# Letting convolution taps in by a backlog meter, and resting buffer rings behind their stores, in a four-layer image kernel

## The chip, the cores and the metric

The kernel runs on one core of one Trainium2 chip. The metric is the device time of one execution in microseconds (us), as the median of several runs. A core has five engines that work from queues of their own, each in order: PE (matrix products and transposes), DVE (vector operations), ACT (activations, copies), POOL (elementwise work) and SP. Nearly all DMAs of this kernel, loads and stores alike, are issued from SP's queue. Data lie in SBUF, sums of products in PSUM, and intermediate images in DRAM.

## The reference

The input is four images of 384 channels and 48 x 48 pixels (2304 tokens), all float32. Four residual layers follow each other, each on the group-normalised image:

```python
x = x + _L0_conv_ref(_gn(x), ...)   # Mamba block: in-projection, causal conv of 4 taps, SiLU,
                                    # scan h = dA*h + dBx over 2304 tokens for 768 channels x 16 states,
                                    # y = sum_s h*C + xin*D, gate by SiLU(z), out-projection, layer norm
x = x + _L1_conv_ref(_gn(x), ...)   # 1x1 conv, filter in the DFT of 8x8 patches,
                                    # depthwise 3x3 conv (9 taps), gelu(x1)*x2, 1x1 conv
x = x + _L2_conv_ref(_gn(x), ...)   # depthwise 11x11 conv, kernels made of 4 points
x = x + _L3_conv_ref(_gn(x), ...)   # 4 experts (two 1x1 convs each), top-2 gate per pixel
```

Where every expert is picked first and second somewhere in the batch, the weights of the top 2 become 1, so that the usual case of layer 3 is the plain sum of the four experts; a branch at the end (`weighted`) does the general case and is not taken with these inputs.

## The kernel before, in words

The scan of layer 0 sets the clock of the program. Each image is cut into 5 chunks of tokens (`CHUNKS`, 460 or 464), each chunk into 6 blocks of 128 channels times 16 states: 96 scans of 128 x 460 per chunk, 1920 in all. The loop `for u in range(N + 6)` in `scans` emits one scan per **slot** `u` under `tc.manual_schedule()`, so each engine's instructions stand in the order in which the loop writes them. In each slot stand: ACT's `decay` two or three slots ahead (da = exp(dt*A), in PSUM), POOL's `drive` three slots ahead (bu = u*B), DVE's `scan`, and the product with C. The product is on DVE in a "fast" slot (`product_now`) and on POOL in a "slow" one (`product`); after the first image's chunks, slots with `u % 4 < 2` are slow. PE then adds the 16 states up by transposing (`turned`). B and C of two slots are broadcast from DRAM to all partitions by one DMA each (`spread`, SP; 3 buffers for B, 4 for C).

All other work is written as generators (`Task`) that yield what they will do next: `("pe", weight, (ring, 1))`, `("act",)`, `("dve",)`, `("late",)`, `("pool",)`. A `Lane` steps its tasks three times per slot: phase 0 (act), 1 (pe, dve, pool), 2 (late). A `Meter` holds PE's work: its value falls by 2.3 us per slot, and a step of a nonzero weight is let in only up to 3.7. A `Ring` stands for a set of buffers; its oldest buffer counts as free as soon as `done` was called, which is when the last instruction that uses it has been emitted.

The lanes are `aux` (layer 0's own projections and layer norms, planned by slot), `start` (z of images 2 and 3, early), `one` (layers 1 and 2 and the scores of layer 3, `later`) and `two` (`experts` of layer 3). Layers 1 to 3 of image b run beside the scans of image b+1, from slot 480(b+1)+42 on. So the first 480 slots carry layer 0 alone, the last image's layers 1 to 3 come after the scans, and what is left of image 2's experts is done there too. That last part is called the **tail** here; in it the slot loop is no longer tied to scans.

Parts that the change touches:

- `taps` in `finish_strip` (layer 1, L1400 to L1420): nine taps per 128 channels of a strip of 8 image rows (24 strips in all images), 27 taps a strip, each one DVE instruction of 128 x 384. It lets 2 taps into a slot, 3 if the slot is slow.
- `block` (layer 3): one expert on 144 tokens, two products of 9 matmul calls. Image strips come as `xe` from `x3d`, the running sum as `ye` from `y3d`. For the first expert the sum is written over `xe`; later ones write over `ye`. Both rings have 2 buffers during the scans. The store (L1791) is emitted in the slot after its DVE add.
- `windows` and `load_band` (layer 2): bands of `xb` from `x2d` (L1513), stored to `x3d` (L1582), 2 buffers.
- `residual` (L1095) stores layer 0's result out of `xch`, and `load` (L731) refills the other tile of that name for the next chunk. `early_z` (L661) stores z from 3 buffers.
- `begin1` loads layer 1's output weights for each image in two parts.

Of the kernel before, what the change touches and what calls it, by code (L numbers as in the profile page):

```python
# [9 lines left out]
F32 = mybir.dt.float32  # L10
# [32 lines left out]

class Ring:


    def __init__(self, make, n):
        self.make, self.n, self.read = make, n, []

    def free(self, k=1):  # L50
        return all(self.read[: max(0, len(self.read) + k - self.n)])
# [6 lines left out]
    def done(self, k):  # L58
        self.read[k] = True


class Meter:


    def __init__(self, each, limit):
        self.each, self.limit, self.value = each, limit, 0.0

    def slot(self, given):
        self.value = max(0.0, self.value - self.each) + given
# [25 lines left out]
class Lane:  # L95
# [7 lines left out]
    def step(self, phase, slot, at=0):  # L103
        for task in self.active:
            if task.ended:
                continue
            kind, weight, ring, when = task.next
            if PHASE.get(kind, 1) != phase or task.after > slot:
                continue
            if weight and self.bound and self.meter.value + weight > self.meter.limit:  # L110
                continue
            if (ring and not ring[0].free(ring[1])) or (when and not when()):
                continue
            self.meter.value += weight
            task.move(slot)
        self.active = [t for t in self.active if not t.ended]
        while (
            self.queue and len(self.active) < self.width and self.queue[0].at <= max(at, slot)
            and all(t.ended for t in self.queue[0].needs)
        ):  # L120
            task = self.queue.pop(0)
            task.move()
            if not task.ended:
                self.active.append(task)

    def drain(self, slot, others=()):
        n = 0
        while self.queue or self.active:
            self.meter.value = 0.0
            for phase in range(3):  # L130
                for lane in (self, *others):
                    lane.step(phase, slot + n, 1 << 30)
            n += 1
            assert n < 20000, "stuck"
# [8 lines left out]
def tile_layers(ctx: ExitStack, tc: tile.TileContext, a: dict, out: bass.AP):  # L143
# [22 lines left out]
    gexp = const("gexp", [GROUPS, C], a["c_gexp"])  # L166
# [8 lines left out]
    def group_norm(st, bank, mean, rstd, name):  # L175

        mv = small.tile([P, CT, 2], F32, name=f"mv{name}", tag="mv")
        for ct in range(CT):
            nc.vector.bn_aggr(mv[:, ct, :], st[:, ct].rearrange("p k s -> p (k s)"))

        def to_groups(src, n, what):
            ps = bank(f"g{what}{name}")
            for ct in range(CT):
                nc.tensor.matmul(
                    ps[:GROUPS, :n], lhsT=gsel[:, ct, :], rhs=src(ct),
                    start=ct == 0, stop=ct == CT - 1,
                )
            return ps[:GROUPS, :n]

        def to_channels(src, n, what):  # L190
            ps = bank(f"c{what}{name}")
            for ct in range(CT):
                nc.tensor.matmul(
                    ps[:, n * ct : n * ct + n], lhsT=gexp[:, bass.ts(ct, P)], rhs=src,
                    start=True, stop=True,
                )
            return ps[:, : n * CT]

        grp = small.tile([GROUPS, 2], F32, name=f"grp{name}", tag="grp")
        nc.vector.tensor_copy(grp, to_groups(lambda ct: mv[:, ct, :], 2, "m"))  # L200
        nc.vector.tensor_copy(mean, to_channels(grp[:, 0:1], 1, "m"))
        dev = small.tile([P, CT], F32, name=f"dev{name}", tag="dev")
        nc.vector.tensor_sub(dev, mv[:, :, 0], mean)
        nc.vector.tensor_mul(dev, dev, dev)
        var = small.tile([GROUPS, 1], F32, name=f"var{name}", tag="var")
        nc.vector.scalar_tensor_tensor(
            var, to_groups(lambda ct: dev[:, ct : ct + 1], 1, "v"), GN_EPS, grp[:, 1:2],
            ALU.add, ALU.add,
        )
        nc.gpsimd.tensor_tensor(var, var, neghalf[:GROUPS, 0:1], ALU.pow)  # L210
        nc.vector.tensor_copy(rstd, to_channels(var, 1, "v"))

    def group_norm_steps(st, ring, mean, rstd, name):
# [15 lines left out]
        def to_channels(src, n, what):  # L229
            ps, k = ring.take(f"c{what}{name}")  # L230
            for ct in range(CT):
                nc.tensor.matmul(
                    ps[:, n * ct : n * ct + n], lhsT=gexp[:, bass.ts(ct, P)], rhs=src,
                    start=True, stop=True,
                )
            return ps[:, : n * CT], k
# [179 lines left out]
    with ExitStack() as first:  # L416
# [55 lines left out]
        stats0 = wp.tile([P, 2, CT, 2, 3, 6], F32, name="stats0")  # L472
# [86 lines left out]
        def scans(wk, mm, ring, meter, place, lanes, begin):  # L559
# [9 lines left out]
            def image_stats(b, ct, h):  # L569
# [4 lines left out]
                for k in range(3):  # L574
                    yield ("dve",)
                    nc.vector.bn_stats(stats0[:, b % 2, ct, h, k, :], t[:, bass.ts(k, LB)])

            def image_norm(b):
                yield from group_norm_steps(
                    stats0[:, b % 2].rearrange("p c h k s -> p c (h k) s"), ring,  # L580
# [4 lines left out]
            def early_stats(b, ct, h):  # L585
# [6 lines left out]
                for k3 in range(3):  # L592
                    yield ("dve",)
# [9 lines left out]
            def early_fold(b):  # L603
# [21 lines left out]
                yield ("dve",)  # L625
# [11 lines left out]
            def early_z(b, t, j):  # L637
# [22 lines left out]
                yield ("pool",)  # L660
# [28 lines left out]
            def fold(b, which):  # L689
# [22 lines left out]
                yield ("dve",)  # L712
# [12 lines left out]
            def load(i):  # L725
                (b, t), c = G[i], st[i]
# [8 lines left out]
                return  # L735
                yield

            def project(i, j):
# [27 lines left out]
                yield ("dve",)  # L766
# [74 lines left out]
            def steps(i, p):  # L841
# [22 lines left out]
                yield ("dve",)  # L864
# [146 lines left out]
            def gate(i, m):  # L1011
# [9 lines left out]
                yield ("late",)  # L1021
# [4 lines left out]
            def out_proj(i, k):  # L1026
# [20 lines left out]
                yield ("dve",)  # L1047
# [4 lines left out]
            def layer_norm(i):  # L1052
# [8 lines left out]
                yield ("dve",)  # L1061
# [12 lines left out]
            def residual(i, ct):  # L1074
# [14 lines left out]
                yield ("dve",)  # L1089
# [4 lines left out]
                yield ("pool",)  # L1094
# [81 lines left out]
            for tag, shape, n in (  # L1176
# [7 lines left out]
                    n,  # L1184
# [14 lines left out]
            with tc.manual_schedule():  # L1199
# [10 lines left out]
                for u in range(N + 6):  # L1210
# [17 lines left out]
                    meter.slot(0.44)  # L1228
                    soon = u % PAIR >= 8
# [25 lines left out]
                while aux.queue or aux.active:  # L1255
                    at += 1
                    meter.slot(0.0)
                    for phase in range(3):
# [5 lines left out]

        def slow_slot():
            return place[0] % 4 < 2

        def later(b, ring, accr):
# [11 lines left out]
            def slots(tag, shape, n):  # L1280

                return Ring(
                    lambda name: d["wk"].tile(shape, F32, name=name, tag=tag, bufs=n), n
# [11 lines left out]
            def begin1():  # L1295
# [3 lines left out]
                w = d["w_out"] = wk.tile([P, 2, C], F32, name=f"w_out1_{b}", tag="w_out", bufs=1)  # L1299
                nc.sync.dma_start(w[:, 0, :], a["L1_w_outT"][:P, :])  # L1300
                nc.sync.dma_start(w[64:P, 1, :], a["L1_w_outT"][P:, :])
# [38 lines left out]
            def patches(hb, wb):  # L1340
# [24 lines left out]
                yield ("late",)  # L1365
# [27 lines left out]
            def finish_strip(hb):  # L1393
# [7 lines left out]
                def taps(ct):  # L1401
# [3 lines left out]
                    room = 3 if slow_slot() else 2  # L1405
                    for k in range(9):
                        if not room:
                            yield ("dve",)
                            room = 3 if slow_slot() else 2
                        room -= 1  # L1410
# [18 lines left out]
                yield ("dve",)  # L1429
# [6 lines left out]
                yield ("dve",)  # L1436
# [3 lines left out]
                for ct in range(CT):  # L1440
# [3 lines left out]
                        ps[:, :LB], lhsT=w[:, 0, bass.ts(ct, P)], rhs=act[:, 0, :],  # L1444
# [3 lines left out]
                        ps[:, :LB], lhsT=w[64:P, 1, bass.ts(ct, P)], rhs=act[64:P, 1, :],  # L1448
                        start=False, stop=True,
                    )  # L1450
                    yield ("late",)
# [26 lines left out]
            xbs = slots("xb", [P, max(BANDS) * W], 2)  # L1478
# [68 lines left out]
            def windows(ct, k, r, first, last, final):  # L1547
# [26 lines left out]
                if last:  # L1574
                    yield ("late",)
# [5 lines left out]
                    yield ("pool",)  # L1581
# [40 lines left out]
            xg = slots("xg", [P, CT, LB], 2)  # L1622

            def begin3():
# [16 lines left out]
                yield ("dve",)  # L1641
# [4 lines left out]
            def scores_of(hb):  # L1646
# [23 lines left out]
                yield ("dve",)  # L1670
# [17 lines left out]
        def experts(b, ring, rings):  # L1688
# [15 lines left out]
            def begin(e):  # L1704
# [21 lines left out]
                yield ("late",)  # L1726
# [4 lines left out]
            def load3(s, e):  # L1731
                yield (
                    "pool", 0, None,
                    lambda: rings["xe"].free() and (not e or rings["ye"].free()),
                )
                x = take(("x", s, e), "xe", f"xe{b}_{s}_{e}")
                nc.sync.dma_start(x, strip(x3d[b], bass.ts(s, EB)))
                if e:
                    y = take(("y", s, e), "ye", f"ye{b}_{s}_{e}")
                    nc.sync.dma_start(y, strip(y3d, bass.ts(s, EB)))  # L1740
                yield from wait(3)

            def block(s, e):
# [33 lines left out]
                yield ("late",)  # L1777
                key = ("y" if e else "x", s, e)
                x = d[key][0]
                if e:  # L1780
                    y = x.rearrange("p c t -> p (c t)")
                    nc.vector.tensor_add(y, ps[:, : CT * EB], y)  # L1782
                else:
                    for m in range(CT):
                        nc.vector.scalar_tensor_tensor(
                            x[:, m, :], ps[:, bass.ts(m, EB)], b2_sum[:, m : m + 1],
                            x[:, m, :], ALU.add, ALU.add,
                        )
                ring.done(r)
                yield ("pool",)  # L1790
                nc.sync.dma_start(strip(out[b] if e == NE - 1 else y3d, bass.ts(s, EB)), x)  # L1791
                done(key)
# [106 lines left out]
        def of_experts(pool, sizes):  # L1899
            for tag, n in sizes.items():  # L1900
# [5 lines left out]
                    n,  # L1906
# [11 lines left out]
        meter = Meter(2.3, 3.7)  # L1918
        one, two = Lane(8, meter), Lane(4, meter)

        def begin(b):
# [10 lines left out]
            {"we": 1, "xe": 2, "ye": 2, "hr": 1},  # L1932
        )
        with (
# [7 lines left out]
            while not all(ring.read):  # L1942
# [6 lines left out]
        with (  # L1949
# [4 lines left out]
            of_experts(wk, {"we": 2, "xe": 3, "ye": 3, "hr": 3})  # L1954

            one.queue += later(NB - 1, ring, accr)
            while one.queue or one.active or two.queue or two.active:
                at += 1
                meter.slot(0.0)
                if not (one.queue or one.active):  # L1960
# [124 lines left out]
```

## Time and profile before

| | us |
|---|---|
| median of 3 runs | 5413.93 (5412.89 to 5417.67) |
| profiled execution, whole | 5405.14 |
| its span, first to last instruction | 5403.1 |
| first and last scan start | 86.5 and 4515.3 |

| engine | busy us | share of the span |
|---|---|---|
| PE, matmuls | 4646.1 | 86% |
| PE, weight loads | 3666.7 | 68% |
| DVE | 4067.1 | 75% |
| POOL | 3363.1 | 62% |
| ACT | 2989.0 | 55% |

A share of the whole span mixes stages of different limits, so the profile is read by stage here: a stretch with layer 1's taps, one with layer 2, one with experts, and the tail. The trace's record of the 1920 scans on DVE also gives each slot its place in time: slot u begins where the u-th scan starts. From slot 384 to 480, with layer 0 alone, a slot took 1.95 us; over the 96 slots from 1056 on it took 2.85 us.

### The profile page before, as it was taken

How to read it: one execution, taken by the hardware profiler on the slowest of the kernel's cores; microseconds unless marked ns; L12 is line 12 of the kernel's file. 1: busy time of each engine (PE TensorE's matmuls, PEld its weight loads, DVE VectorE, ACT ScalarE, POOL GpSimd, SP SyncE). 2: the span in 40 equal slices, each digit the busy share in tenths (PEclk: the TensorE clock that was granted, in tenths of full speed). 3: DMA queues.
4: the chain of work that ended last, by engine and by line, in shares of the span. 5: the costliest groups of instructions: out<-in, count | busy, mean ns of one | idle time of the engine just before them, and what ended most of it. 6: DMA issues, size and time to landing. Idle time of an engine off the chain costs nothing. (4 is left out here: it accounts for less than half of the span.)

```text
span 5403.1 us, 82006 instructions
## 1 busy us (share of the span) xinstructions
PE 4646.1 (86%) x27796; PEld 3666.7 (68%) x27796; DVE 4067.1 (75%) x5581; ACT 2989.0 (55%) x6632; POOL 3363.1 (62%) x3020
## 2 busy tenths in 40 slices
PE   5898877787768988888889988888799988999899
PEld 3555545454446766765668867665678877889799
DVE  5998899889997888889887778798987875452200
ACT  3566655565547765565567745565477653335321
POOL 3788778886677788876678678775677783000000
PEclk8898987788879999998899999998899999999899
DMA  4565545443344555655566565655566573543210
GB/s 152 172 187 175 178 128 150 129 143 120 111 127 131 148 165 157 191 161 147 149 172 178 161 200 155 173 146 149 154 182 174 158 213 115 175 138 105 64 27 23
DMA packets 648873, 794.36 MB, mean 147 GB/s; under 512 B 60149, under 2 KB 642661, under 8 KB 648062
## 3 DMA queue, kind: packets, MB, share of 16 engines
q1 hardware_dynamic: 638148, 787.38, 49.9%
q8 instruction: 221, 3.62, 0.3%
q10 hardware_dynamic: 10298, 1.67, 0.2%
q14 instruction: 206, 1.69, 0.1%
HBM read 685.04 MB, written 103.81 MB: 146 GB/s over the span
## 5 line engine op out<-in xcount | busy, mean ns | idle before, releaser
L953 POOL TENSOR_TENSOR bu<-u,B 128x460 f32<-128x460 f32 (+1 forms) x1920 | 2227.0, 1170 | 795.5 <-DVE g L966 349.8
L942 ACT ACTIVATE da<-dt,a_neg 128x460 f32<-128x460 f32 (+1 forms) x1920 | 1242.4, 648 | 310.6 <-DVE g L986 185.6
L886 PE MATMUL y<-ident,g 128*115 128x128 f32 (+1 forms) x7680 | 1111.3, 292 | 192.5 <-DVE g L986 114.8
L886 PEld LDWEIGHTS y<-ident,g 128*115 128x115 f32 (+1 forms) x7680 | 991.2, 183 | 400.4 <-DVE g L986 140.5
L995 POOL TENSOR_TENSOR g<-g,C 128x460 f32<-128x460 f32 (+1 forms) x885 | 1030.0, 1164 | 246.8 <-ACT carry L980 244.3
L966 DVE TENSOR_TENSOR_SCAN da<-da,carry,bu 128x460 f32<-128x460 f32 (+1 forms) x828 | 971.7, 1174 | 122.2 <-ACT da L942 76.7
L966 DVE TENSOR_TENSOR_SCAN g<-da,carry,bu 128x460 f32<-128x460 f32 (+1 forms) x708 | 819.8, 1167 | 57.7 <-issue 18.8
L986 DVE TENSOR_TENSOR g<-da,C 128x460 f32<-128x460 f32 (+1 forms) x1035 | 656.4, 634 | 175.7 <-DMA C<-bcd 62.0
L980 ACT COPY carry<-da 128x1 f32<-128x1 f32 x828 | 130.3, 157 | 760.5 <-DVE g L986 758.0
L1750 PE MATMUL pout<-hr,we 128*128 128x144 f32 x3456 | 485.0, 297 | 51.5 <-ACT hr L1766 37.8
L1750 PE MATMUL ph<-xe,we 128*128 128x144 f32 x3456 | 484.7, 298 | 33.6 <-DMA xe<-x3d 18.9
L1750 PEld LDWEIGHTS pout<-hr,we 128*128 128x128 f32 x3456 | 456.3, 197 | 75.3 <-ACT hr L1766 47.9
L1750 PEld LDWEIGHTS ph<-xe,we 128*128 128x128 f32 x3456 | 459.4, 199 | 51.5 <-DMA xe<-x3d 13.7
L1557 PE MATMUL pc<-band,row 128*128 128x162 f32 (+14 forms) x3456 | 451.3, 284 | 11.2 <-ACT row L1544 10.9
L1557 PEld LDWEIGHTS pc<-band,row 128*128 128x128 f32 x3456 | 440.0, 194 | 16.6 <-ACT row L1544 11.9
L749 PE MATMUL pin<-xch,w_inx 128*128 128x463 f32 (+2 forms) x720 | 344.8, 621 | 55.1 <-DMA xch<-in_x 32.3
L1415 DVE SCALAR_TENSOR_TENSOR dw<-pad,w_dw,dw 128x384 f32<-128x384 f32 x576 | 348.0, 615 | 20.4 <-ACT pad L1390 9.6
L1037 PE MATMUL po<-w_out,zs 128*115 128x384 f32 (+1 forms) x960 | 342.2, 499 | 14.7 <-DVE ye L1782 9.3
L1766 ACT ACTIVATE hr<-ph,nb 128x144 f32<-128x144 f32 x576 | 176.2, 376 | 279.2 <-PE ph L1750 278.4
L1524 ACT ACTIVATE rep<-x,br,wr 128x192 f32<-128x192 f32 x576 | 273.7, 540 | 4.2 <-issue 4.2
L768 DVE SCALAR_TENSOR_TENSOR xc<-pin,conv_w,xc 128x460 f32<-128x460 f32 (+1 forms) x360 | 249.2, 692 | 30.7 <-ACT xc L762 18.5
L749 PEld LDWEIGHTS pin<-xch,w_inx 128*128 128x128 f32 x720 | 143.8, 213 | 179.8 <-issue 136.3
(211 smaller groups left out, 5979.2 us busy)
## 6 DMA issues: line engine op xcount, KB each, us to landing
B<-bcd SPq DMA_DIRECT2D x768, 230.0 KB, 3.6
C<-bcd SPq DMA_DIRECT2D x768, 230.0 KB, 4.0
B<-bcd SPq DMA_DIRECT2D x192, 232.0 KB, 3.8
C<-bcd SPq DMA_DIRECT2D x192, 232.0 KB, 4.3
xe<-x3d SPq DMA_DIRECT2D x192, 216.0 KB, 2.8
ye<-y3d SPq DMA_DIRECT2D x144, 216.0 KB, 2.8
y3d<-ye SPq DMA_DIRECT2D x96, 216.0 KB, 2.2
xs<-x1d SPq DMA_DIRECT2D x24, 576.0 KB, 5.2
```

The source lines that it names most:

```text
L749: nc.tensor.matmul(ps[:, lo : halo + n], lhsT=w_inx[:, k, bass.ts(j, P)], rhs=c["x"][:, k, lo : halo + n], start=k == 0, stop=k == CT - 1,)
L886: nc.tensor.matmul(c["y", m][:w, bass.ts(k, P)], lhsT=src[:, bass.ts(k, w)], rhs=ident, is_transpose=True, start=c["terms", m] == 1 and k ...
L942: nc.scalar.activation(da[:, :n], c["dt", p][:, m % 2, :n], AF.Exp, scale=a_neg[:, m, s : s + 1])
L953: nc.gpsimd.tensor_mul(bu[:, :n], c["u", p][:, m % 2, :n], live["B", u // 2][:, :n])
L966: nc.vector.tensor_tensor_scan(here[:, :n], da[:, :n], bu[:, :n], last if t else nil[:, 0:1], ALU.mult, ALU.add,)
L986: nc.vector.tensor_mul(live["g", u][:, :n], live["h", u][:, :n], live["C", u // 2][:, :n])
L995: nc.gpsimd.tensor_mul(g[:, :n], g[:, :n], live["C", u // 2][:, :n])
L1037: nc.tensor.matmul(ps[:w, :C], lhsT=c["zs"][:, m, bass.ts(k, w)], rhs=w_out0[:, m, :], start=m == 0, stop=m == MT - 1,)
L1415: nc.vector.scalar_tensor_tensor(v, src, w_dw[:, ct, k : k + 1], v, ALU.mult, ALU.add)
L1524: nc.scalar.activation(rep[:, :, n, :, :].rearrange("p g r c -> p r g c"), rows.rearrange("p (r g c) -> p r g c", r=BR, c=BC), AF.Identity ...
L1557: nc.tensor.matmul(d["acc2"][0][:, : BANDS[k] * W].rearrange("p (h w) -> p h w", w=W)[:, lo - edges[k] : hi - edges[k], xlo:xhi], lhsT=d[" ...
L1750: nc.tensor.matmul(ps[:, bass.ts(m, EB)], lhsT=w[:, k, bass.ts(m, P)], rhs=of[:, k, :], start=k == 0, stop=k == CT - 1,)
```

## The change

It has four parts.

1. A second meter, `meter.vector`, counts DVE's work. It falls by 2.4 per slot, not under -1.2, and gains 1.17 in a slow slot (the scan) and 1.74 in a fast one (scan and product). Steps of kind dve and late now carry weights and add to it when they run, but they are not held back by it. Only `taps` asks it: a tap goes in while the value and 0.57 stay within 3.4, otherwise the task waits for the next slot.
2. A ring may rest: `done` records the slot, and the buffer is free `rest` slots later. `xb` 2, `xg` 1, the rings of `early` 2, and during the scans `xe` 1 and `ye` 2.
3. Stores are emitted later: `yield from wait(2)` or `wait(3)` in place of one `("pool",)`. `load` waits 2 slots; `load3` waits 2 after its loads where it waited 3.
4. Buffers: `ye` has 3 (2 before), `xb` 4 (2); the first expert now writes its sum to a `ye` tile, not over `xe`, so that no store reads `xe`. `stats0` has one part instead of two. The second half of layer 1's output weights is kept for all images in rows 64 to 127 of the constant `gexp`, loaded once from ACT's queue, and is not loaded again per image.

```diff
 class Ring:
-    def __init__(self, make, n):
-        self.make, self.n, self.read = make, n, []
+    def __init__(self, make, n, rest=0):
+        self.make, self.n, self.read, self.rest = make, n, [], rest
     def free(self, k=1):
-        return all(self.read[: max(0, len(self.read) + k - self.n)])
+        return all(
+            v is not False and v + self.rest <= CLOCK[0]
+            for v in self.read[: max(0, len(self.read) + k - self.n)]
+        )
...
     def done(self, k):
-        self.read[k] = True
+        self.read[k] = CLOCK[0]
 class Meter:
...
     def slot(self, given):
-        self.value = max(0.0, self.value - self.each) + given
+        self.value = max(self.least, self.value - self.each) + given
+    def admits(self, weight):
+        return self.value + weight <= self.limit
 class Lane:
...
-            if weight and self.bound and self.meter.value + weight > self.meter.limit:
+            meter = self.meter if kind == "pe" else self.meter.vector
+            if kind == "pe" and weight and self.bound and not meter.admits(weight):
                 continue
...
-            self.meter.value += weight
+            meter.value += weight
...
     # early_z
-                yield ("pool",)
+                yield from wait(2)
                 nc.sync.dma_start(zd[b][...], z[:, :n])
...
     # load(i)
+                yield from wait(2)
...
     # residual
-                yield ("pool",)
+                yield from wait(3)
                 nc.sync.dma_start(x1d[b][...], x)
...
     # the slot loop of scans
                     meter.slot(0.44)
+                    meter.vector.slot(0.0 if u >= N else 1.17 if where(u)[4] else 1.74)
...
     # begin1
-                w = d["w_out"] = wk.tile([P, 2, C], ...)
-                nc.sync.dma_start(w[:, 0, :], a["L1_w_outT"][:P, :])
-                nc.sync.dma_start(w[64:P, 1, :], a["L1_w_outT"][P:, :])
+                w = d["w_out"] = wk.tile([P, C], ...)
+                nc.sync.dma_start(w, a["L1_w_outT"][:P, :])
...
     # taps
-                    room = 3 if slow_slot() else 2
                     for k in range(9):
-                        if not room:
+                        while not meter.vector.admits(0.57):
                             yield ("dve",)
-                            room = 3 if slow_slot() else 2
-                        room -= 1
+                        meter.vector.value += 0.57
...
-            xbs = slots("xb", [P, max(BANDS) * W], 2)
+            xbs = slots("xb", [P, max(BANDS) * W], 4, 2)
...
     # windows, after the DVE add
-                    yield ("pool",)
+                    yield from wait(2)
                     nc.sync.dma_start(x3d[b][of_band(ct, k)], x[:, :n])
                     xbs.done(xk)
...
-            xg = slots("xg", [P, CT, LB], 2)
+            xg = slots("xg", [P, CT, LB], 2, 1)
...
             def load3(s, e):
                 yield (
                     "pool", 0, None,
-                    lambda: rings["xe"].free() and (not e or rings["ye"].free()),
+                    lambda: rings["xe"].free() and rings["ye"].free(),
                 )
                 x = take(("x", s, e), "xe", ...)
                 nc.sync.dma_start(x, strip(x3d[b], bass.ts(s, EB)))
+                y = take(("y", s, e), "ye", ...)
                 if e:
-                    y = take(("y", s, e), "ye", ...)
                     nc.sync.dma_start(y, strip(y3d, bass.ts(s, EB)))
-                yield from wait(3)
+                yield from wait(2)
...
     # block, the end
-                yield ("pool",)
-                nc.sync.dma_start(strip(out[b] if e == NE - 1 else y3d, bass.ts(s, EB)), x)
-                done(key)
+                yield from wait(2)
+                nc.sync.dma_start(strip(out[b] if e == NE - 1 else y3d, bass.ts(s, EB)), y)
+                done(("y", s, e))
...
         meter = Meter(2.3, 3.7)
+        meter.vector = Meter(2.4, 3.4, -1.2)
...
-            {"we": 1, "xe": 2, "ye": 2, "hr": 1},
+            {"we": 1, "xe": 2, "ye": 3, "hr": 1}, {"xe": 1, "ye": 2},
```

## The prediction

> **What bounds the kernel now.** I read the page's first part, then a table of stages (busy time of each engine in chosen stretches), then SP's waits, the waits of DVE and POOL, and a timeline of one stall.
>
> ```profile
> PE 4646.1 (86%) x27796; PEld 3666.7 (68%) x27796; DVE 4067.1 (75%) x5581; ACT 2989.0 (55%) x6632; POOL 3363.1 (62%) x3020
> ```
>
> No engine is full over the span. By stage (columns: stretch, its length, busy us of PE, PEld, DVE, ACT, POOL, clock, DMA share, GB/s):
>
> ```profile
> 2400.00:2640.00 240.00, 199.12 (x982) 144.17 (x983) 217.79 (x314) 128.02 (x284) 152.02 (x138) 0.86 0.49 146
> ...
> 3124.00:3345.00 221.00, 194.64 (x1238) 155.85 (x1237) 174.64 (x232) 114.70 (x210) 172.93 (x154) 0.95 0.61 178
> ...
> 4515.00:5100.00 585.00, 539.39 (x3764) 474.92 (x3762) 211.42 (x437) 222.82 (x525) 4.25 (x14) 0.96 0.43 123
> 5100.00:5403.00 303.00, 297.39 (x2368) 297.18 (x2367) 17.79 (x62) 59.28 (x193) 0.00 (x0) 0.97 0.08 22
> ```
>
> The first row is a stretch with layer 1's taps: DVE is busy 91% and sets the pace. The second has experts beside the scans: DVE 79%, POOL 78%, PE 88% in a modelled figure and 71% by weight loads. Nothing is full there, so waits set the pace. The last two are the tail: PE alone. Now SP's waits:
>
> ```profile
> SPq L930 <- POOL bu L953: 1759.8, 649, 12.1
> ...
> SPq L1740 <- DMA y3d<-ye: 244.6, 92, 7.5
> SPq L1791 <- DVE ye L1782: 240.2, 91, 7.6
> SPq L1737 <- DMA y3d<-xe: 156.8, 47, 8.0
> SPq L1513 <- DMA x3d<-xb: 139.0, 52, 5.6
> ```
>
> The first is harmless pacing (B waits for its buffer). The others stop the whole queue: a load waits until the store out of its buffer has landed, or a store waits for DVE's add. What stands behind them is B and C. One case, SP first, then POOL, then DVE:
>
> ```profile
> 2984.91 0.44 SPq L1582 DMA_DIRECT2D x3d<-xb  x1
> 2989.91 0.32 SPq L1513 DMA_DIRECT2D xb<-x2d  x1
> 2990.32 0.39 SPq L1791 DMA_DIRECT2D out<-ye  x1
> 2990.76 0.48 SPq L1737 DMA_DIRECT2D xe<-x3d  x1
> 2995.31 0.36 SPq L1740 DMA_DIRECT2D ye<-y3d  x1
> 2995.76 0.44 SPq L930 DMA_DIRECT2D B<-bcd  x1
> ```
> ```profile
> 2999.77 1.15 POOL L953 TENSOR_TENSOR bu<-u,B 128x460 f32<-128x460 f32 x1 [7.22 <-DMA B<-bcd]
> ```
> ```profile
> 3001.19 0.64 DVE L986 TENSOR_TENSOR g<-da,C 128x460 f32<-128x460 f32 x1 [5.81 <-DMA C<-bcd]
> ```
>
> The store at 2984.91 is followed at once by the refill of its buffer: 5.0 us blocked; then 4.6 us more for ye. B leaves 9 us late and POOL and DVE both stand. In sum, over the whole trace:
>
> ```profile
> POOL bu L953 <- DMA B<-bcd: 98.2, 49, 7.2
> ...
> DVE g L986 <- DMA C<-bcd: 62.0, 28, 6.1
> ```
>
> **The change part by part.** Positions come from the two built instruction orders, counted by slot, times from the trace. The sum is made on the profiled execution (5405.14 us); the median of the runs is 8.8 us above it, and I carry the difference over to the median.
>
> *1. Taps.* No tap is added or removed (648 at 615 ns, row L1415). They spread: slots 565-702, 1046-1177 and 1526-1657 become 565-744, 1046-1252 and 1526-1729, that is 42, 75 and 72 slots more. Layers 2 and 3 follow later by as much. DVE's mean load by row durations (which overlap by about 0.2 us a slot) falls from 2.81 us per slot to 2.45 in slots 1104 to 1152, the fullest before. So a slot in the tap stretch gets shorter, about by what the added slots cost. What is gained is only idle time of DVE: in the tap row it is 22 us in 240 (0.24 per slot of about 2.6 us), in the expert row 46 in 221 (0.49 per slot of 2.34 us), of which about 0.15 are DMA stalls that part 2 takes. So 147 slots of images 1 and 2 go from 0.34 to 0.24 idle: 15 us. The bursts come on top: DVE's load over 4 slots spreads by 0.26 us in place of 0.50, and two waits of 6.7 us each in which a tap stood behind ACT's SiLU (DVE dw L1413 <- ACT act L1422: 13.5, 2) move elsewhere. I take 22 us, bounds 0 and 45. For image 0's 42 slots I take nothing: idle there is 0.19 per slot already.
>
> *2. SP's queue.* In the order before, all 96 loads of ye in the scans stand in the same slot as the newest expert store, all 19 refills of xch in that of the store out of layer 0's tile, all 52 of xb in that of the band store. After: ye at least 2 slots later, xch 2, xb at least 4. Two slots are 4.7 us against landings of 2.2 (y3d), 3.2 (x3d), 4.2 us (x1d). And no store reads xe any more. So L1740's 244.6 us, L1737's 156.8 and L1513's 139.0 go nearly whole, the waits for DVE (L1791, L1582, L661) mostly. What is late next on SP: the refill of xr (L1398 <- DMA x2d<-xr, 67.0), unchanged. Most of this was hidden by the lead of B (4 slots) and C (5). On the timeline I merge waits of any engine for a DMA in the scans, those less than 4 us apart counted once: 165 us, of which 128 follow within 13 us of more than 3 us of blocked SP. POOL catches up part of it (78% busy), DVE none of its C waits. I take 0.85 removed times 0.53 on the path: 58 us, bounds 10 and 128.
>
> Here a rule speaks against the change. The Trainium skill's page "DMA: Bandwidth & Descriptors", section "Rules for kernel authors", tells to issue a DMA early and to wait for it late; part 2 issues every store 1 or 2 slots later and xch 2 slots later. By the rule the 19 refills of xch lose up to 2 x 2.35 us each, 89 us on PE, which already waits for them (PE pin L749 <- DMA xch<-in_x: 32.3, 10). The trace says that the early place buys nothing, as the queue is in order and the load stood still for the store's 4.2 us. I go by the trace, put xch at nothing, and keep 30 us of loss in the range.
>
> *3. The tail.* Image 2's experts begin at slot 1946, not 1894, so 64 blocks lie in the tail where 56 did. A block is 36 matmuls; at 0.126 us each (297.39 us for 2368 in the last row) that is 4.5 us, 8 of them 36 us. With part of image 2's scores (6.7) and a begin (2) PE gets 45 us more where it is the bound. Taken off: about 8 us of the hole at the start of layer 2, now covered by blocks. Loss 37 us, bounds 28 and 64 (the upper with nearly 20 us idle at the joint, since the weights of image 2's first expert, landing in 5.9 and 7.2 us, are asked for only after the scans; out-projection and scores, 28 us of PE, should cover them). The scans lose the blocks' adds on DVE: 5 us gained.
>
> *4. Rest.* One output-weight load per image less, one more from ACT's queue at the start: nothing, hidden by the 86.5 us before the first scan, at worst 1 us. z of images 2 and 3 spreads from slots 59-289 to 63-352: PE has 1.7 us per slot there under DVE's 1.83, nothing. No POOL compute is moved except by slots; stores pass SP only. The weights on dve and late steps hold back nothing.
>
> Sum: -22 - 58 - 5 + 37 = -48 us; 5413.9 - 48 = 5366.
>
> A second rule, from the Trainium skill's page "Perfetto Trace Analysis", section "Identifying the Most-Contended Engine", ranks by occupancy, for PE by weight loads. That puts DVE (75%) before PE (68%); since no DVE work goes, it would promise nothing from parts 1 and 2 and not see part 3. The stage rows disagree: weight loads are 297.18 of 303 us at the end, and in the expert row nobody is full.
>
> **The rivals.** *Tail wins (slower).* 45 us of PE work plus up to 20 us at the joint land where nothing hides them, while the SP stalls turn out to be absorbed by POOL's three bu buffers and idle moves elsewhere. For: PE is the only engine in the tail. Against: DVE's C waits have no such cover. With parts 1 and 2 giving 20 us and the tail +55: 5449. It decides from the point where the scans save less than 37 us.
>
> *Even.* The SP stalls are half hidden (20), taps bring 15, tail 37: 5414.
>
> *Large gain.* Each SP stall also holds ACT's carry and PE's sums; all 128 us go, taps 30, tail 30: 5286. For: the idle of 0.49 per slot in the expert stretch has no busy engine behind it. Against: a third of it is ACT late for da, which stays.
>
> That the ordering effect is absent is excluded by the slots above.
>
> **How the numbers follow.** Forecast (about 5325 to 5395) 0.5, large gain 0.15, even 0.15, tail 0.2. Some 0.2%, or 10.8 us, is what a measurement can tell. Faster 0.65, same 0.15, slower 0.2. The range takes in most of the large gain and half of the slow case: 5300 to 5436.
>
> **What would show it.** Right: L1740, L1737 and L1513 gone from SP's waits for stores; B and C waits together under 70 us; the last scan starting near 4430 us (4515.3 before); from there to the end some 925 us (888). Part 1 is right if tap stretches take about 2.5 us a slot and idle stays near 0.2. Wrong: B and C waits gone and the last scan still after 4480, meaning the stalls were covered or PE or ACT took their place; or a tail over 950 us.

## The result, and the profile after

| | before | after |
|---|---|---|
| median, us | 5408.37 (5399.42 to 5421.59, 8 runs) | 5431.17 (5420.78 to 5439.36, 8 runs) |
| last scan starts at, us (profiled execution) | 4515.3 | 4529.1 |
| from there to the end, us | 887.9 | 908.2 |

The changed kernel takes 1.0041 times as long, with a 95% interval of 1.0026 to 1.0055: slower by some 23 us, where 48 us of gain were forecast. Its profiled execution took 5439.36 us (span 5437.2), the slowest of its eight; that of before took 5405.14.

The first part of its page, busy time by engine:

```profile
PE 4641.9 (85%) x27796; PEld 3670.0 (67%) x27796; DVE 4055.6 (75%) x5581; ACT 2988.0 (55%) x6632; POOL 3362.4 (62%) x3020
```

Every busy time is within 12 us of that before. No engine works more, so some engine must wait more. The queue of SP (engine and line, what it waited for: us in total, times, longest) became much as promised. The refill's row of before stands first, the rows of after follow:

```profile
SPq L731 <- DMA x1d<-xch: 72.8, 19, 5.3
```
```profile
SPq L944 <- POOL bu L967: 2495.3, 851, 14.0
...
SPq L1801 <- DVE ye L1791: 144.4, 70, 8.2
...
SPq L1750 <- DMA y3d<-ye: 80.8, 46, 6.5
...
SPq L747 <- DMA x1d<-xch: 20.6, 11, 4.1
SPq L1523 <- DMA x3d<-xb: 15.1, 9, 3.9
```

The loads of ye waited 244.6 us for stores, now 80.8; those of xb 139.0, now 15.1; those of xe no longer stand behind a store at all. The refill of xch (L747) waited 72.8 us for the store of layer 0's result (L731 before), now 20.6. And what had stood behind them, B and C, comes in time. POOL's waits for a DMA:

```profile
POOL bu L967 <- DMA C<-bcd: 10.8, 7, 2.8
POOL bu L967 <- DMA B<-bcd: 4.2, 3, 1.7
```

B cost POOL 98.2 us before; DVE's wait for C, 62.0 us before, is 3.0. So the waits that carried the forecast went, and yet the last scan starts 14 us later. PE's waits say where to look; the refill's row of before stands first, then the two largest rows of after:

```profile
PE pin L749 <- DMA xch<-in_x: 32.3, 10, 6.3
```
```profile
PE y L900 <- DVE g L1000: 112.4, 81, 10.1
PE pin L763 <- DMA xch<-in_x: 104.2, 17, 10.1
```

The first of after was 114.8 us before and is no news. The second grew from 32.3 to 104.2 us: layer 0's in-projection waits for the refill of xch. DVE's wait at the next step, xc from ACT, grew as well (before, then after):

```profile
DVE xc L768 <- ACT xc L762: 18.5, 22, 4.2
```
```profile
DVE xc L782 <- ACT xc L776: 82.1, 37, 7.8
```

The longest of these 17 stalls in the timeline of after (start, length, what runs; in brackets, how long the engine had been idle and for what), SP first, then PE, ACT and DVE:

```profile
1159.84 0.50 SPq L1109 DMA_DIRECT2D x1d<-xch  x1
1162.45 0.33 SPq L944 DMA_DIRECT2D B<-bcd  x1
1162.82 0.43 SPq L944 DMA_DIRECT2D C<-bcd  x1
1166.17 0.38 SPq L747 DMA_DIRECT2D xch<-in_x  x1
```
```profile
1159.55 1.13 PE L900 MATMUL y<-ident,g 128*115 128x128 f32 x8
1170.76 4.95 PE L763 MATMUL pin<-xch,w_inx 128*128 128x463 f32 x6 [10.08 <-DMA xch<-in_x]
```
```profile
1175.74 0.73 ACT L776 ACTIVATE xc<-pin,cb,conv_w 128x460 f32<-128x460 f32 x1 [11.11 <-PE pin L763]
```
```profile
1163.81 1.18 DVE L980 TENSOR_TENSOR_SCAN da<-da,nil,bu 128x460 f32<-128x460 f32 x1
1176.50 0.16 DVE L262 COPY mean<-cm 128x3 f32<-128x3 f32 x1 [11.50 <-PE cm L247]
```

The refill leaves SP at 1166.17 and its data are there 4.6 us later, when PE starts at once. But PE had come to the in-projection at 1160.68, 5.5 us before the refill was even issued. ACT's xc stands behind PE, and DVE, whose queue is in order, stands behind both, so that for 11.5 us there is no scan. The refill is asked for later than its user comes.

The slots show when the time is lost. Subtracting the starts of the scans in both traces, after is 42 us late by slot 530, at the end of the stretch that carries layer 0 alone, before any tap or expert. It arises mostly in the first half of the chunks of 96 slots (slots 96 to 144 took 1.86 us each before and 2.05 after, slots 480 to 528 1.92 and 2.06). Some 12 of the 42 us are not the refill's: a_noxch below, with the refill early, is that late there too. Then the stretches with taps win it back: between slots 1056 and 1152 the lag falls from 51 to 16 us, between 1536 and 1632 from 18 to -12. At slot 1872 the two are level, at the last scan after is 14 us late, and the tail adds 20. The tap stretch and the tail in the table of stages (stretch, length, busy us of PE, PEld, DVE, ACT, POOL, clock, DMA share, GB/s):

```profile
2500.00:2740.00 240.00, 211.09 (x1277) 169.83 (x1276) 220.39 (x307) 142.48 (x330) 172.67 (x156) 0.94 0.58 167
...
4529.00:5120.00 591.00, 569.59 (x4042) 496.87 (x4040) 207.16 (x427) 232.16 (x551) 5.84 (x16) 0.99 0.45 133
5120.00:5437.00 317.00, 301.25 (x2378) 301.03 (x2378) 28.01 (x98) 59.44 (x193) 0.00 (x0) 0.95 0.08 21
```

In the tap stretch DVE is still the bound, at 92%, with fewer taps in each slot: 97 slots begin in these 240 us, 84 in the row of before. The last two rows hold 6420 matmuls where before's two held 6132: 288 more, 8 blocks of 36. PE is busy 870.8 us in them, 34 more than before, and idle 37, which is 14 less, so that they are 20 us longer together.

### The profile page after: what moved, and what is told of

Same layout as the page of the kernel before. It is cut to its first block, busy times and chain, and to the rows that moved or that the text cites. A ratio compares the mean times of both kernels' runs of the same rounds, so it can differ in the third digit from the quotient of the medians.

```text
span 5437.2 us, 81947 instructions
## 1 busy us (share of the span) xinstructions
PE 4641.9 (85%) x27796; PEld 3670.0 (67%) x27796; DVE 4055.6 (75%) x5581; ACT 2988.0 (55%) x6632; POOL 3362.4 (62%) x3020
## 5 line engine op out<-in xcount | busy, mean ns | idle before, releaser
L900 PEld LDWEIGHTS y<-ident,g 128*115 128x115 f32 (+1 forms) x7680 | 1002.2, 185 | 423.7 <-issue 155.0
L763 PE MATMUL pin<-xch,w_inx 128*128 128x463 f32 (+2 forms) x720 | 345.6, 622 | 112.9 <-DMA xch<-in_x 104.2
```

The source lines that it names most:

```text
L763: nc.tensor.matmul(ps[:, lo : halo + n], lhsT=w_inx[:, k, bass.ts(j, P)], rhs=c["x"][:, k, lo : halo + n], start=k == 0, stop=k == CT - 1,)
L900: nc.tensor.matmul(c["y", m][:w, bass.ts(k, P)], lhsT=src[:, bass.ts(k, w)], rhs=ident, is_transpose=True, start=c["terms", m] == 1 and k ...
```

## The experiments

The theory, A in the expectations: the refill of xch is issued too late for the projections, whose start is fixed by slot, and PE's wait for it is lost time one for one. The rivals are that the taps' spreading and the longer tail ate the gain, and that the resting rings put a new wait in place of the old ones. Each kernel was timed beside before, which came out near 5412 us each time; ratios are to before, with the 95% interval. The last two columns are of the profiled execution. Its time lay within 4 us of the median but for four kernels: 8 us above it in after and a_noxch, 13 above in b_taps, 10 below in b_rings.

| kernel | median us | ratio | last scan at | tail |
|---|---|---|---|---|
| after | 5431.17 | 1.0041 [1.0026, 1.0055] | 4529.1 | 908.2 |
| a_noxch | 5337.21 | 0.9858 [0.9843, 0.9873] | 4439.7 | 903.5 |
| b_xch | 5537.68 | 1.0232 [1.0218, 1.0246] | 4644.8 | 887.5 |
| a_resid | 5399.43 | 0.9977 [0.9968, 0.9987] | 4486.0 | 912.4 |
| a_lead | 5346.96 | 0.9877 [0.9862, 0.9893] | 4437.5 | 908.0 |
| b_taps | 5368.23 | 0.9916 [0.9903, 0.993] | 4467.3 | 912.5 |
| b_rings | 5350.86 | 0.9891 [0.9875, 0.9906] | 4495.0 | 843.8 |
| r_experts | 5335.92 | 0.9864 [0.9849, 0.9879] | 4490.1 | 841.7 |
| n_each26 | 5370.39 | 0.9921 [0.9908, 0.9935] | 4494.4 | 875.0 |
| n_each28 | 5345.55 | 0.9877 [0.9861, 0.9893] | 4502.7 | 840.3 |
| p_468 | 5369.67 | 0.9926 [0.9913, 0.994] | 4495.7 | 872.1 |
| t_experts | 5327.89 | 0.9834 [0.9821, 0.9848] | 4421.8 | 905.2 |

### After with the refill as before, and before with the refill of after

```diff
# a_noxch, against after        # b_xch is the reverse, against before
     # load
-    yield from wait(2)
     # residual
-    yield from wait(3)
+    yield ("pool",)
```

> The changed kernel with the refill of layer 0's input tile as before: residual's store one step after its add, load without its two waits. Theory A (late refill): the change moves each of the 19 refills not by two slots but by four (slot 140 in place of 136 and so on), because residual now ends three steps later and load waits two more, while the projections that read the tile still start at slot 45 of the chunk; PE stands 104.2 us for it where it stood 32.3, DVE's convolution behind it. Then this kernel gains 40 to 70 us on the changed one: about 5370 to 5390, faster than before by 20 to 40, and the waits of pin for the refill fall back to about 32 us. Rival B (tail and experts): the refill is hidden as the prediction held, and the loss is the 20 us more of the tail and the joint before it: then this kernel stays within 10 us of the changed one (5431).

> The kernel before with only the refill of the input tile late: residual's store after three steps, load after two more. Theory A: it loses 40 to 70 us (5450 to 5480), the loss sits in the first half of each chunk of 96 slots, and pin waits about 100 us for the refill. Rival B: within 10 us of before.

These two lines cost the change 94 us (5431.2 to 5337.2; 99 by the two ratios to before): all else of it gains 75 us. Put into before alone they cost 125 us. Both are larger than the 40 to 70 us that I had expected of theory A. The waits of PE for the refill in a_noxch and in b_xch, and those of SP in a_noxch:

```profile
PE pin L764 <- DMA xch<-in_x: 9.6, 6, 2.6
```
```profile
PE pin L748 <- DMA xch<-in_x: 161.0, 18, 20.1
```
```profile
SPq L746 <- DMA x1d<-xch: 69.6, 20, 5.3
```

In a_noxch PE waits 9.6 us for refills, and SP stands 69.6 us at L746 again, as it did in before, without harm. In b_xch a single wait reaches 20.1 us, since there the late refill also stands in the queue that still stops for stores: SP stood from 3539.8 to 3546.1 us for a store out of xe, and the refill left at 3548.1. The rivals that the taps, the tail or the resting rings made the kernel slower are out: a_noxch has all of them.

Why four slots, where I had counted two? `load` begins when the tasks of `residual` have ended. With `wait(3)` these end two slots later, and then comes `load`'s own `wait(2)`. So the refill does stand two slots behind the store, as the prediction counted, but four behind its old place. In the orders of instructions the refill stands at slots 40, 136, 232 and so on before, and at 44 of each chunk (140, 236, 332) after. The projections start at slot 45 of a chunk in both, `put(45 + 3 * j, ("x", more, j), ...)`. The lead fell from five slots to one, about 1.9 us where layer 0 is alone, and the landing took 4.6 us in the stall above. In the traces the refills leave SP in slots 138, 234 and 330 before, as SP still stands for the store there, and in 141, 237 and 333 after.

### Half of the delay, and all of it with later projections

```diff
# a_resid, against after: only load's wait goes; the refill stands at slot 42
     # load
-    yield from wait(2)
# a_lead, against after: the refill stays at slot 44
-                            put(45 + 3 * j, ("x", more, j), lambda j=j: project(more, j),
+                            put(49 + 2 * j, ("x", more, j), lambda j=j: project(more, j),
```

> The changed kernel with the two waits of load taken out, residual's store still three steps after its add: the refill is emitted at slot 42 of the chunk, two later than before, lead 3 slots of some 2 us. It lands in 4.5 to 6 us, so theory A lets the wait of pin fall from 104 us to between 35 and 70, and the time to 5365 to 5400, so that the loss is steep over the last two slots. If the loss grows evenly with the slots, half of 94 us: about 5385.

> The changed kernel as it is, refill at its late slot 44 of the chunk, but layer 0's projections start at 49 and follow every 2 slots (before: from 45, every 3), so that the refill has its five slots of lead again. If what costs is the lead alone (theory A), nearly all of the 94 us between this and the kernel with the early refill comes back, less what the crowded projections and a later SiLU cost: 5345 to 5375. If the late store or the late refill itself costs (by what stands on SP's queue), it stays above 5410.

With three slots of lead in place of one, PE and SP wait in a_resid

```profile
PE pin L764 <- DMA xch<-in_x: 73.0, 15, 10.0
```
```profile
SPq L746 <- DMA x1d<-xch: 75.0, 21, 5.7
```

and the time falls by 32 us; the step from slot 42 to 40 is worth 62 more. My expectation of a loss that is steep over the last two slots (42 to 44) missed: it is the first two that cost most, and PE's wait of 73.0 us lies just over the 70 named. SP's row shows why: in a_resid the refill stands in the slot of its store again and stands still for it, 75.0 us in all where after has 20.6, so that in the trace it leaves SP in slots 141, 237 and 332, hardly earlier than in after. With the refill as late as in after but the projections four slots later at the start, denser after it, the time of a_lead is 5347 us, and PE's wait for the refill is 0.9 us. So it is the lead that costs, not where the refill stands in SP's queue.

The price can be read off. From a_noxch to after PE's wait for the refill grows by 104.2 - 9.6 = 94.6 us and the time by 94.0; from a_noxch to a_resid by 73.0 - 9.6 = 63.4 and 62.2; from before to b_xch by 161.0 - 32.3 = 128.7 and 125.3. That is one for one in three pairs of medians, in a kernel whose PE is busy 85% of the span; the profiled executions give 94, 55 and 129 us.

### The taps alone, and the rings alone

```diff
# b_taps, against before: the second meter, its weights, part 4's stats0 and gexp, and in taps
-                    room = 3 if slow_slot() else 2
-                        if not room:
+                        while not meter.vector.admits(0.57):
...
# b_rings, against a_noxch: the same lines of taps put back
```

> The kernel before with the DVE meter and the taps under it, no ring that rests, stores and buffers as before, refill as before. By the prediction's step 1 and 3: scans 22 us shorter plus 5, tail 37 longer: +10 us, about 5418. Theory A says nothing else. Rival C (the meter itself is the loss): the slower taps push the experts out and this kernel alone is 20 us or more slower than before.

> The changed kernel with taps let in two or three to a slot as before and the refill as before: rings that rest, later stores, three ye buffers and four xb buffers alone. By the prediction's step 2: 58 us faster than before (bounds 10 and 128), about 5350; the waits for B and C fall under 70 us together; and as 50 blocks lie in its tail where 56 did, up to 25 us more. Rival D (SP's stalls were covered): within 10 us of before although SP's waits for landings are gone.

b_taps was to be slower by 10 us by the terms of my sum (-22 - 5 + 37) and is faster by 44. In its profiled execution, which is 24 us faster than that of before, the last scan starts 48 us earlier and the tail is 25 us longer. Part of the surplus can be seen. With SP's queue as before, still stopping for stores, DVE's wait for C fell from 62.0 us to

```profile
DVE g L1001 <- DMA C<-bcd: 32.6, 18, 5.8
```

and POOL's wait for B from 98.2 to 75.6: together 52 us of the DMA waits that I had booked to the rings went when the taps were spread.

b_rings was to gain 58 us and gains 61.5. But its last scan starts only 20 us earlier, and its tail is 44 us shorter; by the order of instructions 50 blocks are left for the tail where 56 were, some 27 us of PE at 4.5 us a block. SP's waits in it:

```profile
SPq L1756 <- DMA y3d<-ye: 70.8, 37, 7.0
...
SPq L1529 <- DMA x3d<-xb: 17.1, 11, 2.8
```

Alone the two parts gain 105 us, together (a_noxch) 75. The profiled executions show where the 30 us go. In the scans nothing is lost: the last scan starts 48 and 20 us earlier alone, 76 together. It is the tail: 25 us longer and 44 shorter alone, and together 16 longer. The rings shorten the tail mainly by letting blocks run before it, and with the meter at 2.4 no block of image 2 does: all 64 (1152 matmuls of `ph`) come after the last scan's start in a_noxch as in b_taps. Nor is part 4, which both kernels have, a gain of the scans that is counted twice: r_experts below has it too and is 9 us behind before still at slot 1300.

### Which rings

```diff
# r_experts, against before: layer 3's rings (and part 4, the meter without the taps)
-            {"we": 1, "xe": 2, "ye": 2, "hr": 1},
+            {"we": 1, "xe": 2, "ye": 3, "hr": 1}, {"xe": 1, "ye": 2},
     # load3: xe and ye both asked for, y taken for the first expert too
-                yield from wait(3)
+                yield from wait(2)
...
     # block: the sum goes to ye for every expert
-                yield ("pool",)
-                nc.sync.dma_start(strip(out[b] if e == NE - 1 else y3d, bass.ts(s, EB)), x)
+                yield from wait(2)
+                nc.sync.dma_start(strip(out[b] if e == NE - 1 else y3d, bass.ts(s, EB)), y)
```

> The kernel before with the experts' part of the rings alone: ye 3 buffers that rest 2 slots, xe resting 1, the first expert's sum in ye, stores two slots after the add, the block two slots after its load. Taps, refill, bands and z as before. It leaves 49.5 blocks in the tail, as the kernel with all rings does (50). If the rings' 61 us come from the experts (their stores and reloads stopped SP's queue and slowed them), this one gains 45 to 65 us (5348 to 5368) and most of it in the tail; if from the bands and z stores, under 25 us (over 5387).

The experts' edit alone gains 76 us, more than all rings together; in the profiled executions 25 of it lie in the scans and 46 in the tail. It is more than the removal of stops: a block may also begin a slot sooner after its load, and `ye` has a third buffer, and no run parts these. SP's waits in it, with layer 2's bands as in before, and those of POOL and DVE for B and C:

```profile
SPq L1529 <- DMA x3d<-xb: 133.0, 52, 5.9
```
```profile
POOL bu L968 <- DMA B<-bcd: 24.4, 13, 3.3
```
```profile
DVE g L1001 <- DMA C<-bcd: 19.3, 7, 6.1
```

SP still stops 133 us for the bands' stores, but POOL and DVE wait only 24.4 and 19.3 us for what stands behind it (98.2 and 62.0 before). Most of these stops are thus hidden, though this row looks like those of ye and xe. Taking them away together with the rest of the rings (xg, z of the early images) gained nothing: b_rings is 15 us slower by the medians, 7 by the profiled executions, and the intervals of the two ratios just meet. Whether one of the other rings has a cost that hides a gain of the bands stays open.

### How fast the meter should run

```diff
# against a_noxch
-        meter.vector = Meter(2.4, 3.4, -1.2)
+        meter.vector = Meter(2.6, 3.4, -1.2)    # n_each26; 2.8 in n_each28
...
+            meter.vector.each = (2.4, 2.6, 2.8)[b - 1]    # p_468: one rate for each image
```

> The changed kernel with the early refill and the DVE meter falling by 2.6 per slot, not 2.4: taps end 30 to 50 slots earlier (slots 715, 1201, 1681), and 58 blocks lie in the tail, not 64. If the meter gains by spreading taps over slots in which DVE would idle (prediction's step 1), the scans lose part of their gain (20 us) and the tail wins 26: 5325 to 5340. If it gains by cutting bursts, the scans keep it and the time is about 5315.

> The same with 2.8 per slot: the taps' stretches are as short as before the change (to slots 693, 1180, 1660), 50.5 blocks in the tail, yet no burst is let in over the limit. By spreading alone nothing would be left of the meter: equal to the kernel with rings alone, 5351. By cutting bursts: 10 to 25 us under it, 5325 to 5340.

> The changed kernel with the early refill, and the DVE meter falling by 2.4 per slot while image 0's layers run, 2.6 for image 1's, 2.8 from image 2's on, so that fewer blocks (57.5, not 64) are left for the tail. If taps only trade idle time in the scans against PE work in the tail, the scans lose about 20 us on the early-refill kernel and the tail wins about 25: 5325 to 5340, the same within the error. If the tail can be had for less, 5310 to 5325.

A faster meter lets more taps into a slot, layer 1 takes fewer slots, and more of the experts should be done before the tail. At 2.8 the trade is plain: the last scan starts 63 us later than at 2.4 (4502.7 and 4439.7), the tail is 63 us shorter (840.3 and 903.5), and the profiled time is the same (by the medians 8 us longer). And with 5345.6 us it is as good as no meter in the taps (b_rings, 5350.9): beside the rings, smoothing bursts without spreading the taps over more slots gains about nothing. But 2.6 and the mixed rates came out some 30 us worse than either end. Both expectations missed: against a_noxch they lose 55 and 56 us of the scans' gain, nearly as much as 2.8 does, and win only 28 and 31 us in the tail, with 58 blocks in it against 50.5 at 2.8. In n_each26 DVE stands 7.5 us twice for a GELU of layer 1 that ACT runs behind layer 0's SiLU; in p_468 the longest such wait is 2.1 us. The cause is open.

### The taps with the experts' rings

```diff
# t_experts, against r_experts
-                    room = 3 if slow_slot() else 2
-                        if not room:
+                        while not meter.vector.admits(0.57):
...
```

> The experts' rings of the change and its DVE meter at 2.4 per slot, with refill, bands, gate scores and z stores as before. Each alone gains: rings of the experts 76 us, meter 44. If both add up, 5292; if, as with all the rings, some 30 us are lost between them since both draw on the same idle time and 64 blocks lie in the tail, 5315 to 5330. If bands and z stores cost as little as 15 us in the kernel with the early refill (5337) too, 5322.

At 5327.89 us (5314.71 to 5333.55) this beats both kernels: 0.9834 [0.9821, 0.9848] of before. The sum of its two parts alone would be 120 us; it gets 85. Here too the loss is in the tail alone: its last scan starts 94 us earlier than before's (48 and 25 in the parts), at 4421.8, the earliest of all, and its tail of 905.2 us, 17 over before's, is the long one of the spread taps (25 longer and 46 shorter in the parts). The refill, the bands and z stand as in before; part 4 is in it.

## Why the prediction was wrong, point by point

**The step that failed is in part 2: "xch 2 slots later" and "put xch at nothing".** What was put at 0 cost 94 us, which turned a forecast gain into a loss. The step has two errors. The count was of `load`'s own wait, that is of the distance to the store; that `load` also waits for `residual`, whose end moved too, was missed, and the refill came four slots later than before. And the argument for nothing, that the load stood still behind the store anyway, looked at when SP issues the refill but not at when PE needs it. Before, five slots of some 1.9 us, 9.5 us, just covered standing still (72.8 us in 19 refills, 3.8 each) and a landing of some 4.6; after, one slot of 1.9 us covers neither what is left of the standing still nor the landing. The rule that part 2 weighed there and set aside, from the Trainium skill's page "DMA: Bandwidth & Descriptors", section "Rules for kernel authors" (issue early, wait late), was right: by it 19 refills times 2 x 2.35 us gave an estimate of up to 89 us, and 94 were measured. The closeness is partly luck, since that figure has half the slots and no slack. The 30 us kept in the range were a third of it.

**The rest of part 2** was right in mechanism: most of SP's waits for stores went (ye's 244.6 us became 80.8), and the waits of POOL and DVE for B and C did; what is left of them, 10.8 + 4.2 + 3.0 = 18 us, is well under the 70 us that I named. Its size, 58 us, fits the 61.5 of b_rings, but not for the reason given: in its profiled execution only 20 us were saved in the scans, 44 in the tail, where part 2 had nothing. Of three rows of SP's waits taken as one kind, the edit that removes ye's and xe's gains 76 us, and the removal of xb's adds no gain that these runs show.

**Part 1** was mis-sized. The term of 22 us for taps, with 5 for adds moved, is 48 in b_taps, near the upper bound of 45 for the taps and 5 for the adds. The slot lengths came as named: slots 1056 to 1104 took 2.75 us before and 2.46 after, slots 1584 to 1632 2.98 and 2.60. What it likely left out is that a burst of taps also makes B and C look late, 52 us of waits that I had given to part 2. For the scans as a whole the two errors cancel: parts 1 and 2 with the adds were put at 85 us, and in a_noxch the last scan starts 76 us earlier (4439.7, near the 4430 forecast). That is in part luck.

**Part 3**, +37, was +20 in after (908.2 against 887.9), +16 in a_noxch and +25 in b_taps. The count of 8 blocks was right (288 more matmuls), its price too high: PE's busy time in the tail grew by 34 us where 45 were put, and its idle time fell by 14 where 8 were put.

**Part 4** at nothing was not tested by itself; every run but b_xch has it. The starts of the scans show a small loss. By slot 70 b_taps, r_experts and t_experts, which have part 4 and the old z stores, are 3 to 5 us behind before, and after, a_noxch and b_rings, where z is stored later too, 8 to 9; b_xch, with neither, is not behind. How this comes about was not followed.

**The rivals.** After is slower, but not as "tail wins" said: its scans did not save less because POOL's buffers had absorbed the stalls, and its tail was 20 us longer, not 55. That the last scan would start after 4480 us with B's and C's waits gone was named as the sign of a wrong forecast, "meaning the stalls were covered or PE or ACT took their place". It is the latter: PE's wait for xch. (In the even case -20 - 15 + 37 makes 5416, not 5414; nothing rests on it.)

With -48 and 94 for xch the sum would have been +46; after is at +23, since without xch the change gains 75, not 48. (94 less 75 is 19; the rest is that before came out at 5408.4 us beside after and at 5412.4 beside a_noxch.)

## What to carry to other kernels

When a transfer is delayed, count all of it: the step's own wait, the wait of the task that it is chained to, and then set the landing against the slot at which the first user stands. What a stopped queue costs is read from the waits of the engines for the transfers behind it, not from its own: here 133 us of stops left POOL and DVE with 24.4 and 19.3 us of waits for B and C. When two gains don't add, look at each stage: here both moved the same blocks into or out of the tail. And take a change of many parts apart on the chip: here two of its lines hid a gain of 75 us.

## What the runs showed of the hardware that was not expected

- PE's waits for one transfer cost their full length in three pairs of kernels (94.6, 63.4 and 128.7 us of wait; 94.0, 62.2 and 125.3 us of time), though PE is busy only 138 us of 187 where layer 0 is alone (859 to 1046 us before). In the stall above PE's wait of 10.1 us becomes 11.1 on ACT and 11.5 on DVE, and DVE, busy 170 us of these 187, has little idle time in which to catch up.
- Spreading DVE's taps, with the stores and their buffers as before, took the waits for B and C from 160 to 108 us (b_taps). My reading, not tested further: how late a broadcast looks depends on when its users come for it.
- Gains of 44 and 61.5 us alone made 75 together, 44 and 76 made 85. In the scans they added in full; the loss was in the tail both times.
